# A fused attention and expert kernel: rows of the next units fetched in the middle of a unit, a block's steps further apart, the third stage's tables in later and smaller pieces

## The chip, the cores and the metric

The kernel runs on one core of a Trainium2 chip. The core has five engines with an instruction queue each: PE (TensorE, matmuls and transposes), DVE (VectorE), ACT (ScalarE), POOL (GpSimd) and SP (SyncE, which here only issues DMAs). An engine takes its instructions in the order of the program and waits on semaphores. The metric is the device time of one execution in microseconds; lower is better.

## What is computed

Two layers on x (2048 tokens, 256 features), each with a residual. Layer norms stand ahead of each part. S is 1601 context rows.

```python
# first layer
x += softmax((Q(ln x) K(ctx)^T * tau + delta) / 4) V(ctx) @ Wo.T   # 16 heads of 16
x += expert_w[argmax(router)] (ln x) * max(softmax(router))        # 8 experts, top 1
# second layer
score = ln(x) @ W_a @ ctx^T, only in a window of +-16 around p_t   # rows outside: -1e9
x += tanh(concat(softmax(score) * gauss @ ctx, ln x) @ W_c.T)
x += slot mixing of ln x: 64 slots, top 8 routing, GRU, slot attention
```

## The kernel before

**First stage** (lines 305 to 738) makes the keys, the values and the queries of the first block of 512 tokens.

**Second stage** (lines 740 to 932) is attention. It runs through 16 units: four blocks of 512 tokens (lb) by four groups of four heads (g), `u = lb * 4 + g`. A unit has 13 iterations i, one for each tile of 128 context rows. An iteration has two slots (pl). A slot writes scores of two heads into PSUM with four matmuls (L904), and ACT takes the exponential (L909). An iteration later `weigh` (L866) multiplies the four exponentials with the values into `acc` (L870); after tile 12 of a unit `finish` copies `acc` to `osb` (L808) and adds steps to a list, `later`.

Before a unit's scores are made, the largest score of each query is searched in bfloat16, so that it can be taken off within the score matmul. `look` (L774) is called four times an iteration and places pieces of that search: PE writes one or two groups of 402 scores (L257; a "take" of 1 uses the one-bank buffer `small`, a take of 2 the two-bank buffer `big`), and DVE reduces them to a maximum (L262). The search runs 8 slots ahead (`LEAD`). When its 64 groups are done, `least` and `turned` bring the maxima by PE, ACT and four small DMAs (L292) into rows of `qt`.

Other work goes in between as steps of `later`, one at a time, after an iteration's `weigh`:

- `block(lb)` (L470): the next block's `stats` (layer norm statistics on DVE, the power on POOL, L102), two times `norm` (L107), two times `turned` (four transposes, L240, and a copy), two times `project` (four matmul passes, L498) with `seconds` (two DVE operations, L303, and `store_queries`, four DMAs to DRAM rows, L216); then `residual` on POOL (L601).
- `finish`: `rows` (transposes and a division, L820); after the fourth group also two `turned` and two `out_half` (L845, and the sum into x, L850).
- `bias` once, in unit 0, and `block_0` near the end: the expert stage's first norm and router.

The gap between two steps is set by the length of the list (L919): the next may start 2 slots later when more than 5 steps wait or the step has a second half, otherwise 4. `busy_to` makes `look` use takes of 2 alone for a short time after a step. Block lb+1 is appended at tile 2 of the first unit of block lb (L890).

The rows of queries come back from DRAM by DMA on SP: `fill(u)` (two DMAs into `qt`, two into `ql`) and `fill_search(u)` (two into `qb`). There are three buffers of `qt` and `ql` (`nq = 3`) and two of `qb`. They are issued behind a unit, for the unit three later (L926 to L929).

**Third stage** (lines 935 to 1553): loads on SP and POOL queues (L953 to L988), then experts for blocks of tokens. `experts(lb)` (L1054) makes 16 pairs a block: two experts at a time for a tile of tokens (four matmul passes, L1064, into one of four y banks), added by two DVE operations (L1071). After each pair `aside(3)` advances up to three generators in turn: `front` (the next block's norm, transposes and router), `window` (the tables of the second layer's window, made once from the two numbers `pt` and `slen`), `slots` (the slot parts that do not depend on x), and for each finished block `windowed` and `weights`. `window` runs to its next `yield`: its first piece is ten DVE instructions (L1095 to L1113) and a gather by POOL (L1115), the second makes `posr`, `inr`, `gr`, `negw`, the third `nout`, `ins`, `gs`. Seven empty yields follow, then its matmuls: `eT`, the sum over all rows outside the window (`out_ps`, 13 row tiles, L1177), `oT`, `m` and `ew`.

Of the kernel before, what the change touches and what calls it, by code (L numbers as in the profile page):

```python
# [25 lines left out]
NLB = T // LB  # L26
TPB = LB // P
NS = (S + P - 1) // P
# [3 lines left out]
NG = 4  # L32
# [30 lines left out]
def body(ctx: ExitStack, tc: tile.TileContext, a: dict, out: bass.AP):  # L63
# [41 lines left out]
    def layer_norm_apply(src, dst, i, stats, rows=P):  # L105
        mv, rstd = stats
        nc.vector.tensor_scalar(  # L107
            dst[:, i, :], src[:, i, :], mv[:rows, i, 0:1], rstd[:rows, i : i + 1],
            ALU.subtract, ALU.mult,
        )  # L110
# [69 lines left out]
    with (  # L180
# [9 lines left out]
        nq = 3  # L190
# [42 lines left out]
        def small():  # L233
            return ps_a.tile([P, LB], F32, tag="pa1", name="a1_ps")
# [4 lines left out]
        def turn(ps, src, t, c, n=P):  # L239
            nc.tensor.transpose(ps[:, t * P : (t + 1) * P], src[:, t, c * P : c * P + n], ident)  # L240
# [64 lines left out]
        with (  # L305
# [164 lines left out]
            def block(lb):  # L470

                xb = x_sb[:, lb * TPB : (lb + 1) * TPB, :]

                rstd_of = []

                def stats():
                    rstd_of.append(layer_norm_stats(xb, TPB))

                yield stats
                for half in range(2):  # L480
                    def norm(half=half):
                        for t in range(half * 2, half * 2 + 2):
                            layer_norm_apply(xb, xn, t, rstd_of[0])

                    yield norm
                for c in range(2):
                    def turned(c=c):
                        ps = small()
                        for t in range(TPB):
                            turn(ps, xn, t, c)  # L490
                        nc.scalar.copy(xnT[:, c, :], ps)

                    yield turned
                for n in range(2):
                    def project(n=n):
                        ps = small()
                        for c in range(2):
                            nc.tensor.matmul(  # L498
                                ps, wq[:, c, n * P : (n + 1) * P], xnT[:, c, :],
                                start=c == 0, stop=c == 1,  # L500
                            )
                        b = bq[:, n : n + 1]
                        if lb == 0:
                            (all_parts if n else pick_queries)(ps, b)
                            return
                        for t in (one_two, hi_lo):
                            first_part(t[0], ps, b)

                        def seconds():
                            for t in (one_two, hi_lo):  # L510
                                second_part(t[1], t[0], ps, b)
                            store_queries(lb, n)

                        return seconds

                    yield project
# [82 lines left out]
            def residual(lb):  # L599
                for t in range(lb * TPB, (lb + 1) * TPB):  # L600
                    nc.gpsimd.tensor_tensor(x_sb[:, t, :], x_sb[:, t, :], bo, ALU.add)  # L601

            def fill_search(u):

                lb, g = divmod(u, NG)
                fetch_rows(qb[u % 2], q_rows[1][lb % 2][g // 2], g)

            def fill(u):

                lb, g = divmod(u, NG)  # L610
                rows = q_rows[0][lb % 2][g // 2]
                fetch_rows(qt[u % nq], rows, g)
                for h in range(2):
                    src = head_rows(rows, g, h).rearrange("(e w) l s -> e w l s", w=W)
                    nc.sync.dma_start(
                        raw(ql[u % nq][h * HR : h * HR + W * E : W]), src[:, W - 1]
                    )
# [122 lines left out]
        with (  # L740
# [25 lines left out]
            NU = NLB * NG  # L766

            LEAD, NSL = 8, 2 * NS  # L770
            searches, held, begun = [], [], []
            taken, last, at, busy_to = 0, 1, 0, 0

# [26 lines left out]
            later, free = [], 0  # L800
# [65 lines left out]
            def weigh(u, i, acc, es):  # L866
# [7 lines left out]
                if i == NS - 1:  # L874
                    later.extend(finish(u, acc))

            before = None
            for u in range(NU):
                acc = None
                for i in range(NS):  # L880
                    if (u, i) == (0, 4):
                        later.insert(0, bias)
                    if (u, i) == (0, 1):
                        for lb in range(2, NLB):
                            load_x(nc.sync, lb)
                    if (u, i) == (2, 0):
                        load_experts()
                    if (u, i) == (NU - 3, 2):
                        later.extend(block_0())
                    if u % NG == 0 and i == 2 and u // NG + 1 < NLB:  # L890
                        later.extend(block(u // NG + 1))
                        later.append(lambda lb=u // NG + 1: residual(lb))
                    n = srows(i)
                    es = []
                    assert i or len(begun) >= u, (u, begun)
                    ready = bool(later)
                    for pl in range(2):
                        slot = (u * NS + i) * 2 + pl
                        look(slot)
                        ps = two()  # L900
                        for k, q in enumerate((qt, ql)):
                            for h in range(2):
                                rows = slice(h * HR, h * HR + NROW)
                                nc.tensor.matmul(  # L904
                                    ps[:n, h, :], kt[u % NG][rows, pl, i * P : i * P + n],
                                    q[u % nq][rows, pl, :], start=k == 0, stop=k == 1,
                                )
                        e = esp.tile([P, 2, LB], F32, name="es")
                        nc.scalar.activation(e[:n], ps[:n], AF.Exp)  # L909
                        es.append(e)  # L910
                    look(slot + 0.5)
                    if before is not None:
                        weigh(*before)

                        look(slot)
                    if ready and slot >= free:

                        rest_of_it = later.pop(0)()
                        free = slot + (2 if len(later) > 5 or rest_of_it else 4)  # L919
                        busy_to = at + (9 if rest_of_it else 2)  # L920
                        if rest_of_it:
                            later.insert(0, rest_of_it)
                    if i == 0:
                        acc = ps_o.tile([P, LB], F32, tag="po", name="acc")
                    before = (u, i, acc, es)
                if u + nq < NU:  # L926
                    assert u % NG != 1 or len(later) < 2, (u, len(later))
                    fill(u + nq)
                    fill_search(u + nq)  # L929
            weigh(*before)  # L930
            while later:
                later.pop(0)()
# [5 lines left out]
    slot = ctx.enter_context(tc.tile_pool(name="slot", bufs=1))  # L938
# [152 lines left out]

    def window():

        slen = late.tile([P, 1], F32, name="slen")
        nc.vector.tensor_copy(slen, slen_i)  # L1095
        lo = late.tile([P, 1], F32, name="lo")
# [7 lines left out]
        base_i = late.tile([P, 1], I32, name="base_i")  # L1104
        nc.vector.tensor_copy(base_i, base)
        nc.vector.tensor_copy(base, base_i)

        at_i = late.tile([NW, 1], I32, name="at_i")
        nc.gpsimd.iota(at_i, pattern=[[0, 1]], base=0, channel_multiplier=1)
# [10 lines left out]
        def in_window(pos, n, name):  # L1120

            t = late.tile([P, n], F32, name=name)
            nc.vector.tensor_scalar(t, pos, lo, None, ALU.is_ge)
            nc.vector.scalar_tensor_tensor(t, pos, hi, t, ALU.is_le, ALU.mult)
            return t

        def gauss(pos, n, name):
            t = late.tile([P, n], F32, name=name)
            nc.vector.tensor_scalar_sub(t, pos, pt)
            nc.vector.tensor_tensor(t, t, t, ALU.mult)  # L1130
            nc.scalar.activation(t, t, AF.Exp, scale=-1.0 / 128.0)
            return t
# [4 lines left out]
        posr = late.tile([P, NW], F32, name="posr")  # L1137
        nc.vector.tensor_copy(posr, posr_i)
        nc.vector.tensor_scalar_add(posr, posr, base)
        inr = in_window(posr, NW, "inr")  # L1140
        gr = gauss(posr, NW, "gr")
        neg = late.tile([P, 1, NK], F32, name="negw")
        nc.vector.tensor_scalar(neg[:, 0, :NW], inr, -1.0, 3e38, ALU.add, ALU.mult)
# [9 lines left out]
        nc.gpsimd.iota(row_i, pattern=[[P, NS]], base=0, channel_multiplier=1)  # L1153
        row = late.tile([P, NS], F32, name="row")
        nc.vector.tensor_copy(row, row_i)
        ins = in_window(row, NS, "ins")
        gs = gauss(row, NS, "gs")
        nc.vector.tensor_scalar(ins, ins, -1.0, 1.0, ALU.mult, ALU.add)
# [1 line left out]
        one = late.tile([1, 1], F32, name="one")  # L1160
        nc.gpsimd.memset(one, 1.0)

        for _ in range(7):
            yield
        eT = late.tile([P, 2, NW], F32, name="eT")
        gET = late.tile([P, 2, NK], F32, name="gET")
# [466 lines left out]
```

## Time and profile before

| | before |
|---|---|
| median of three runs | 1055.93 us (1054.44 to 1056.26) |
| the profiled execution's own time | 1057.95 us |
| its span, first to last instruction | 1056.1 us |
| mean granted PE clock | 0.978 |
| busy: PE, DVE, ACT, POOL | 949.2, 745.1, 519.7, 71.8 us |
| chain that ended last | PE 67%, DVE 25%, issue 4%, DMA 2% |
| first stage | 0 to about 93 us |
| attention, first exponential to last `osb` copy | 93.3 to 769.6 us |
| third stage | 769.5 us to the end |

The span is what the profile sees of the core's instructions; the execution's own time is 1.9 us longer. The page's slices show the whole at a glance, each digit a tenth of 26.4 us:

```profile
PE   7788778999988999998899999899979999999885
DVE  6456868888877888877788887875044749585744
PEclk8998999999999999999999999989998999999998
```

PE is busy almost throughout, DVE second. A pass of a float32 matmul is an instruction of its own in the profile, so that a matmul written once in the code counts twice there. "Idle before" in a row names what ended the engine's last wait. A wait on several semaphores is put down to the one that came last.

### The profile page before, as it was taken

The numbers are of one execution on the slowest core, as the hardware profiler recorded it, in microseconds if no ns is written. First come the engines' busy times: TensorE is split into PE (matmuls) and PEld (weight loads), VectorE is DVE, ScalarE is ACT, GpSimd is POOL, SyncE is SP. The second block draws the span as 40 slices with busy tenths as digits, with TensorE's granted clock in tenths as the row PEclk, the third lists the DMA queues.
The fourth block names the chain that finished last, engine by engine and source line by source line (L and its number), as shares of the span: only waits on it lengthen the run. The fifth ranks groups of instructions, "written<-read, shape, count | busy, mean of one in ns | idle before, by whom it ended". The sixth has DMA issues, their size and how long they took to land.

```text
span 1056.1 us, 14900 instructions
## 1 busy us (share of the span) xinstructions
PE 949.2 (90%) x5822; PEld 443.7 (42%) x5822; DVE 745.1 (71%) x1407; ACT 519.7 (49%) x614; POOL 71.8 (7%) x96
## 2 busy tenths in 40 slices
PE   7788778999988999998899999899979999999885
PEld 3234333444443344443343444443334464545543
DVE  6456868888877888877788887875044749585744
ACT  1423556676756666657566766557820012121430
POOL 4000200000010000000000000000030102121210
PEclk8998999999999999999999999989998999999998
DMA  4764721310102201101211011000080000000002
GB/s 161 158 163 94 150 73 46 110 29 2 29 1 79 68 2 28 29 1 39 81 28 29 2 29 29 1 2 1 2 223 7 1 0 1 1 1 0 1 1 80
DMA packets 32277, 46.98 MB, mean 44 GB/s; under 512 B 6411, under 2 KB 21268, under 8 KB 31950
## 3 DMA queue, kind: packets, MB, share of 16 engines
q1 hardware_dynamic: 30478, 43.65, 15.3%
q10 hardware_dynamic: 1232, 1.61, 0.4%
q8 instruction: 46, 0.75, 0.3%
q0 software_dynamic: 496, 0.76, 0.3%
q14 instruction: 25, 0.20, 0.1%
HBM read 26.77 MB, written 14.04 MB: 39 GB/s over the span
## 4 chain that ended last, share of the span: by engine, by line
PE 67%; DVE 25%; issue 4%; DMA 2%; POOL 1%; ACT 1%; SPq 0%; POOLq 0%; DVEq 0%; ACTq 0%
PE acc L870 18%; PE s_ps L904 14%; DVE mx L262 12%; PE a_ps L257 11%; PE y_ps L1064 7%; DVE xn L107 2%; DVE x_sb L1071 2%; PE a_ps L498 2%; DVE ln_stats L96 1%; PE o_ps L1250 1%; PE a_ps L845 1%; PE a_ps L240 1%; PE s_ps L627 1%; PE a_ps L284 1%; PE x_ps L461 1%
## 5 line engine op out<-in xcount | busy, mean ns | idle before, releaser
L262 DVE TENSOR_REDUCE mx<-a_ps 128x2 f32<-128x804 f32 (+1 forms) x637 | 490.9, 806 | 125.6 <-PE a_ps L257 118.9
L909 ACT ACTIVATE es<-s_ps 128x1024 f32<-128x1024 f32 (+1 forms) x416 | 408.3, 1022 | 204.5 <-PE s_ps L904 201.4
L257 PE MATMUL a_ps<-kb,qb 50*128 50x402 bf16 x992 | 219.5, 342 | 49.0 <-DVE mx L262 40.1
L904 PE MATMUL s_ps<-qt,kt 52*128 52x512 f32 (+1 forms) x832 | 238.2, 521 | 1.5 <-DMA qt<-nT 1.4
L870 PE MATMUL acc<-es,v 128*32 128x512 f32 (+1 forms) x1664 | 225.5, 613 | 0.0
L257 PEld LDWEIGHTS <-qb 50*128 50x128 bf16 x1024 | 77.8, 94 | 296.0 <-issue 282.2
L904 PE MATMUL s_ps<-ql,kt 52*128 52x512 f32 (+1 forms) x832 | 191.8, 396 | 0.0
L904 PEld LDWEIGHTS s_ps<-qt,kt 52*128 52x128 f32 (+1 forms) x832 | 98.1, 189 | 32.0 <-ACT es L909 16.7
L904 PEld LDWEIGHTS s_ps<-ql,kt 52*128 52x128 f32 (+1 forms) x832 | 104.0, 187 | 0.7
L1064 PE MATMUL y_ps<-expert_wT_sb,xT 128*128 128x512 f32 x192 | 89.8, 598 | 0.0
L102 POOL TENSOR_TENSOR ln_rstd<-ln_ve,mhalf 128x2 f32<-128x2 f32 (+2 forms) x28 | 21.1, 754 | 754.2 <-DVE ln_ve L100 752.9
L1071 DVE SCALAR_TENSOR_TENSOR x_sb<-y_ps,r_gate,x_sb 128x256 f32<-128x256 f32 x96 | 46.3, 482 | 32.5 <-PE y_ps L1064 30.7
L870 PEld LDWEIGHTS acc<-es,v 128*32 128x32 f32 (+1 forms) x1664 | 33.1, 108 | 42.2 <-issue 40.5
L1064 PEld LDWEIGHTS y_ps<-expert_wT_sb,xT 128*128 128x128 f32 x192 | 34.1, 191 | 31.9 <-issue 30.8
L1027 ACT COPY xT<-tr_ps 128x512 f32<-128x512 f32 (+1 forms) x28 | 13.4, 494 | 53.3 <-PE tr_ps L1024 53.3
L107 DVE TENSOR_SCALAR xn<-x_sb,ln_mv,ln_rstd 128x256 f32<-128x256 f32 x64 | 33.9, 573 | 1.3 <-POOL ln_rstd L102 1.3
L819 DVE RECIPROCAL rec<-a_ps 128x16 f32<-128x16 f32 x16 | 4.0, 252 | 42.6 <-PE a_ps L240 42.6
L1064 PE MATMUL y_ps<-expert_wT_sb,xnT 128*128 128x512 f32 x64 | 32.6, 637 | 0.0
L1024 PE MATMUL tr_ps<-ident,xn 128*128 128x128 f32 x88 | 17.8, 300 | 10.7 <-DVE xn L107 10.7
L96 DVE BATCH_NORM_STATS2 ln_stats<-x_sb 128x6 f32<-128x256 f32 x64 | 23.3, 413 | 3.4 <-POOL x_sb L1258 3.4
L1071 DVE SCALAR_TENSOR_TENSOR x_sb<-y_ps,gate,x_sb 128x256 f32<-128x256 f32 x32 | 15.5, 483 | 14.0 <-PE y_ps L1064 13.3
L997 PE MATMUL busy_ps<-xnT 128*128 128x512 bf16 x95 | 24.2, 387 | 0.0
(347 smaller groups left out, 724.7 us busy)
## 6 DMA issues: line engine op xcount, KB each, us to landing
qt<-q_rows SPq DMA_DIRECT2D x32, 192.0 KB
q_rows<-qhi SPq DMA_DIRECT2D x8, 512.0 KB
qb<-q_rows SPq DMA_DIRECT2D x30, 96.0 KB
kt<-expert_wT_sb SPq DMA_DIRECT2D x24, 100.5 KB
q_rows<-qp SPq DMA_DIRECT2D x8, 256.0 KB
q_rows<-qlo SPq DMA_DIRECT2D x8, 256.0 KB
ql<-q_rows SPq DMA_DIRECT2D x32, 64.0 KB
expert_wT_sb<-in_expert_wT SPq DMA_DIRECT2D x1, 2048.0 KB
```

Source lines behind the costliest of these rows:

```text
L96: nc.vector.bn_stats(stats[:rows, i, :], src[:, i, :])
L102: nc.gpsimd.tensor_tensor(rstd[:rows, :n], ve[:rows, :n], mhalf[:rows, :n], ALU.pow)
L107: nc.vector.tensor_scalar(dst[:, i, :], src[:, i, :], mv[:rows, i, 0:1], rstd[:rows, i : i + 1], ALU.subtract, ALU.mult,)
L257: nc.tensor.matmul(ps[:, k, :CH], qb[u % 2][rows, pl, t * P : (t + 1) * P], kb[g][rows, pl, c * CH : (c + 1) * CH], start=True, stop=True,)
L262: nc.vector.tensor_reduce(flat[:, n : self.n], ps[:, : self.n - n, :CH], AX.X, ALU.max)
L498: nc.tensor.matmul(ps, wq[:, c, n * P : (n + 1) * P], xnT[:, c, :], start=c == 0, stop=c == 1,)
L870: nc.tensor.matmul(acc[HP * j : HP * (j + 1), :], v[:n, i, h * VW : h * VW + HP], es[j // 2][:n, j % 2, :], start=i == 0, stop=i == NS - 1,)
L904: nc.tensor.matmul(ps[:n, h, :], kt[u % NG][rows, pl, i * P : i * P + n], q[u % nq][rows, pl, :], start=k == 0, stop=k == 1,)
L909: nc.scalar.activation(e[:n], ps[:n], AF.Exp)
L997: nc.tensor.matmul(calm[0].rearrange("p e d -> p (e d)"), xnT[:, 1, :P].bitcast(BF16)[:, 1::2], xnT[:, 0, :].bitcast(BF16)[:, 1::2], start ...
L1064: nc.tensor.matmul(ps.rearrange("p e d -> p (e d)"), xT[:, c, tok], ew[:, c, pair * 2 * D : (pair + 1) * 2 * D], start=c == 0, stop=c == 1,)
L1071: nc.vector.scalar_tensor_tensor(xb[:, t, :], ps[:, k, :], gate[:, t, e : e + 1], xb[:, t, :], ALU.mult, ALU.add,)
```

## The change

Three things are changed.

1. `fill` and `fill_search` move from behind a unit to its iteration i = 6, from unit 1 on, and fetch for the unit two later (`u + nq - 1`).
2. The limit above which steps follow each other by 2 slots goes from 5 waiting steps to 9 (`LATE`). Block 1 is appended at tile 8 of unit 0 and not at tile 2; blocks 2 and 3 stay where they were, at tile 2 of units 4 and 8.
3. `window` begins with five empty yields, has four more yields between its pieces, and four instead of seven empty ones ahead of its matmuls.

```diff
-            LEAD, NSL = 8, 2 * NS
+            LEAD, NSL, LATE = 8, 2 * NS, 9
...
+            blocks_at = {(0, 8): 1, (NG, 2): 2, (2 * NG, 2): 3}
...
-                    if u % NG == 0 and i == 2 and u // NG + 1 < NLB:
-                        later.extend(block(u // NG + 1))
-                        later.append(lambda lb=u // NG + 1: residual(lb))
+                    if (u, i) in blocks_at:
+                        lb = blocks_at[u, i]
+                        later.extend(block(lb))
+                        later.append(lambda lb=lb: residual(lb))
+                    if u and i == 6 and u + nq - 1 < NU:
+
+                        assert u % NG != 2 or len(later) < 2, (u, len(later))
+                        fill(u + nq - 1)
+                        fill_search(u + nq - 1)
...
-                        free = slot + (2 if len(later) > 5 or rest_of_it else 4)
+                        free = slot + (2 if len(later) > LATE or rest_of_it else 4)
...
-                if u + nq < NU:
-                    assert u % NG != 1 or len(later) < 2, (u, len(later))
-                    fill(u + nq)
-                    fill_search(u + nq)
...
     def window():
+        for _ in range(5):
+            yield
         slen = late.tile([P, 1], F32, name="slen")
...
         nc.vector.tensor_copy(base, base_i)
+        yield
...
         nc.vector.tensor_scalar_add(posr, posr, base)
+        yield
         inr = in_window(posr, NW, "inr")
+        yield
         gr = gauss(posr, NW, "gr")
...
         nc.vector.tensor_copy(row, row_i)
+        yield
         ins = in_window(row, NS, "ins")
...
-        for _ in range(7):
+        for _ in range(4):
             yield
```

As the changed program is laid out, the steps fall as follows, written as (unit, iteration). Block 1: before, stats at (0,2), norms at (0,3) and (0,5), turned at (0,7) and (0,9), projects at (0,11) and (1,1); after, stats (0,8), norms (0,10) and (0,12), turned (1,1) and (1,3), projects (1,5) and (1,8). Block 2, and block 3 four units on: before, out_half (4,5) and (4,6), stats (4,7), norms (4,8) and (4,9), turned (4,11) and (5,0), projects (5,2) and (5,5), rows (5,10); after, out_half (4,5) and (4,7), stats (4,9), norms (4,11) and (5,0), turned (5,2) and (5,4), projects (5,6) and (5,9), rows (6,1). In the third stage `window`'s first DVE instruction stands behind the sixth pair of the first expert block and not behind the first.

## The prediction, on record before the changed kernel ran

> **What bounds the kernel now.** I read the chain of waits first: PE holds 67% of it and DVE 25%, so PE is the engine to follow and DVE is what stops it. Then I cut the span into stretches, one per attention unit and then the start of the third stage, and looked for the ones where PE is idle. Columns: stretch, length, then busy time with instruction count for PE, PEld, DVE, ACT and POOL, the granted PE clock, DMA share, GB/s.
>
> ```profile
> 93.30:149.90 56.60, 45.70 (x297) 19.69 (x298) 43.21 (x70) 28.52 (x31) 6.74 (x10) 0.94 0.57 118
> ...
> 442.20:488.10 45.90, 42.44 (x311) 20.12 (x309) 36.79 (x61) 27.98 (x31) 4.07 (x5) 1.00 0.07 18
> 488.10:534.20 46.10, 40.97 (x293) 17.48 (x290) 35.11 (x50) 29.61 (x34) 0.00 (x0) 1.00 0.20 69
> ...
> 573.70:611.90 38.20, 36.25 (x284) 16.00 (x281) 32.65 (x48) 26.70 (x29) 0.00 (x0) 1.00 0.08 21
> ...
> 778.00:793.00 15.00, 7.25 (x25) 4.00 (x25) 10.70 (x43) 0.93 (x3) 5.30 (x14) 0.83 1.01 272
> 793.00:797.50 4.50, 4.50 (x10) 2.33 (x10) 1.36 (x4) 0.59 (x1) 0.00 (x0) 0.50 0.00 1
> ```
>
> Row four is unit 11, without a block's steps: PE idle 2.0 of 38.2 us. Rows two and three are units 8 and 9, which carry a block: longer by 7.7 and 7.9 us, but idle only 3.5 and 5.1, so most of their length is the steps' own matmuls. Unit 0 (row one) idles 10.9. The outlier is the fifth row: PE busy 7.25 of 15 us, then 4.5 us at half clock. The timeline there:
>
> ```profile
> 776.72 0.15 DVE L1095 CAST slen<-slen_i 128x1 f32<-128x1 int32 x1 [2.54 <-DMA slen_i<-in_slen]
> ...
> 778.00 0.15 DVE L1097 TENSOR_SCALAR lo<-pt_b 128x1 f32<-128x1 f32 x1 [1.13 <-DMA pt_b<-in_pt]
> ...
> 779.56 1.99 PE L845 MATMUL a_ps<-WoT_sb,aT 128*128 128x256 f32 x8 [1.53 <-DVE x_sb L850]
> ...
> 789.14 0.80 PE L1024 MATMUL tr_ps<-ident,xn 128*128 128x128 f32 x2 [3.72 <-DVE xn L107]
> ...
> 792.45 0.80 PE L1024 MATMUL tr_ps<-ident,xn 128*128 128x128 f32 x2 [2.50 <-DVE xn L107]
> ```
>
> DVE stands in front of two small loads (2.54 and 1.13 us) because window()'s first instructions come early in its queue; the last attention block's L850 is behind them, then the layer norm. PE's three gaps are 1.53, 3.72 and 2.50 us, 7.75 together. The clock records show half speed from 787.9 to 798.1; an expert pair there took 3.41 us in the chain of waits, 1.88 elsewhere.
>
> **Third stage: the later tables.** The piece order of the changed kernel on DVE is now: stats, pair 2, stats, L850, pair 3, L850, two norms, pair 4, two norms, pairs 5 and 6, and only then slen. I walk it with the rows' durations (pair on DVE 1.00, stats of two tiles 1.25, L850 0.69, norm of two tiles 0.73; pair on PE 1.88, L845 group 1.97, four transposes 1.06, router 1.85).
> Until 774.2 nothing differs. DVE: pair 2 to 775.2, stats to 776.5, L850 when PE's first L845 group ends (777.17), so to 778.0. PE's second L845 group starts at 778.05 instead of 779.56 and ends at 780.05. Then pair to 781.9, gate transposes to 782.5, pair to 784.4. The norms need POOL's rstd. POOL issues its thirteen loads until 780.57, clears xn and takes 0.73 us twice: 781.5 and 782.3. DVE: norms to 782.3, pair 4 to 783.3, norms to 784.0, before PE asks at 784.4. From there PE is fed: transposes 785.5, pair 787.3, transposes 788.4, pair 790.2, router to 792.0. Before, the router ended at 801.27. Difference **-9.2 us**: the 7.75 of gaps, and the rest half clock.
> Given back? The tables' PE work (output sum 5.71, the rest 2.7 us) goes from the first expert block into the next, the same amount. Its 26 DVE instructions up to gs sum to 4.9 us; the pieces are 0.4 to 1.2 us beside PE pairs of 1.88, of which DVE uses 1.00. Cover is thus 0.88 per pair and the four y banks lend one or two pairs. Without that cover it would be 4.9 us back. POOL's gather now waits for at_i at about 794, with posr and row queued behind it; POOL's next rstd is needed in the next expert block only. From the third expert block on PE's order is the same, so the gain is carried to the end. I take -9.2, bounds -4.3 and -10.
>
> **Attention: rows fetched in the middle.** fill(u+2) at key tile 6 of unit u replaces fill(u+3) at the end of unit u: the same six DMAs 6.5 tiles later in program order. What releases them is the last matmul on the old qt, at the end of unit u-1, in both. SP's queue shows that they are issued then (unit 5 ends at 364.6; its last use of the old qt is just before 362.2):
>
> ```profile
> 362.23 0.80 SPq L226 DMA_DIRECT2D qt<-q_rows  x2
> 363.12 1.34 SPq L615 DMA_DIRECT2D ql<-q_rows  x2
> 364.52 1.04 SPq L226 DMA_DIRECT2D qb<-q_rows  x2
> ```
>
> SP runs ahead of PE's place, so the issue time stays. What they are moved past on SP: in unit 1 the stores of block 1's queries now come after fill(3), and the four expert loads before fill(4). The experts' 2 MB, issued at 197.5, kept the DMA engines busy to about 204.7, some 7 us; put ahead, fill(4) lands that much later, near 206, and its search starts near 222. In blocks 2 and 3 nT of one search goes ahead of the second store. The cost is 0, hidden by the 18 slots of 1.47 us (26 us) between issue and search. If SP were held at its place in the program, 6 slots (8.8 us) would stay for 4.3 us of issue plus the landing; upper bound 2 us a unit for 13 units.
>
> **Attention: steps further apart.** I measure an iteration from its first acc matmul to the next one's:
>
> ```profile
> 247.23 1.07 PE L870 MATMUL acc<-es,v 128*32 128x512 f32 x8
> ...
> 249.73 1.06 PE L870 MATMUL acc<-es,v 128*32 128x512 f32 x8
> ```
>
> That is 2.50 us. An iteration's search takes sort them: takes of 2,1,2 give this 2.50; 1,2,1 give 2.71; 1,2,1,2 give 3.34; with a step inside, the trace has 3.3 (turned), 4.95 (out_half), 4.12 (stats), 6.13 (project), 3.65 (seconds), 4.26 (a lone norm beside 1,2,1,2). I placed the new order's steps and takes and gave each iteration the length of its like.
> Blocks 2 and 3: tiles (4,6) to (6,12) took 110.6 us. New: unit 4's seven, 2.5+5.0+2.5+5.4+3.2+3.0+2.5 = 24.1; unit 5, with two projects at 6.75 and 6.0, two seconds at 3.65 and two lone turned at 3.4, 46.1; unit 6, now with two rows steps, 39.1. Sum 109.3: -1.3 each. PE's idle time there is 10.7 us, but the 1.2 us that a project and the 1.3 that stats cost are waits of PE for DVE inside that step, and go wherever it goes.
> Block 1: tiles (0,2) to (2,5) took 112.2; new: unit 0 42.0, unit 1 50.7, unit 2's six 18.4, sum 111.1: -1.1.
> Units 13 and 14: the same steps in other tiles, 64.9 before; 61.7 after plus whichever half-clock spells return (4.8 us before): +0.5, between -3 and +1.6. Together **-3.2**, bounds -7 and +2. The new norm and stats places match one row each, which is why these are wide.
>
> **A rule against it.** The Trainium skill, TensorE: Matmul & The Clock Gate, section "HAM oscillation — how this bites in real kernels", says in effect: avoid PE-idle gaps over about 3.4 us. By it only the hole before 793 costs clock, and steps spread over more iterations, each stopping PE for 1.3 us or less, cost none. The trace is harsher: the records show half clock from 678.6 to 682.0, right after one 1.09 us gap behind a lone norm, and that iteration took 4.07 instead of 2.50. By the rule the spread adds 0 and the sum below stays 1043.6; by the row each lone norm or stats adds 1.6, and the change makes about ten such places: 1059.6. But other stretches as idle kept full clock, so I take 0 and put the row into the range.
>
> **The sum.** The profiled execution took 1057.95 us (span 1056.1, 1.9 around it), 2.0 above the median of the runs, 1055.93. -9.2 - 3.2 + 0 = -12.4: 1045.6 against its own time, 1043.6 against the median; I say 1044.
>
> **Rivals.** *Attention gives nothing:* the steps' waits move along and one or two half-clock spells eat the 3.2. For it: PE is already busy for 89 to 92% of block units. Time 1055.9 - 9.2 = 1047. *The tables' stall moves:* at the new place DVE has route and pair work too (0.19 us times seven, plus 0.68 and 1.00, beside one PE pair), so all 4.9 us return. For it: DVE busy 33.1 of 50 us from 830 on. Against: four banks. Time 1055.9 - 4.3 - 3.2 = 1048.4. *Fetch held at its place:* it doesn't do what it says then; it is hidden anyway unless landing takes over 4.5 us. *Slower, by clock:* half-clock spells in the attention stage at 1.6 us (678.6) to 3.2 (699.1, after the router's small matmuls), about 2.4 each. Six more would be 14.4 and turn -12.4 into a loss; seven give 1061. For it: ten new lone places. Against: cut in the clock records' steps of 3.41 us, the attention stage has a dozen stretches with PE busy under 70%, and one such spell.
>
> **How the numbers follow.** Forecast 0.60 (1044); attention nothing 0.17 (1047); stall moves 0.12 (1048); more gained than read 0.04 (1040); slower 0.07. A measurement tells 0.2%, 2.1 us, from no change. The first four make 0.93; of it 0.04 is for both losses with some spells on top, which end between 1054 and 1058: faster 0.89, same 0.04, slower 0.07. The range goes from the likeliest less its bound, 1039.5, to both losses together with one spell, 1051.5.
>
> **What would show it.** Right: no gap over 1 us on PE from 769 to 800, full clock there, router end near 792; blocks' three units within 131 to 129 us; fills issued at the end of the unit before. Wrong: DVE waiting for slen late, half clock in several block units, PE waiting for a DMA on qb or qt, or gaps near the output sum in the second expert block.

## The result, and the profile after

The changed kernel takes 1040.93 us (median of 5 runs, 1038.75 to 1048.27) against 1055.93 (5 runs, 1054.44 to 1058.84): a ratio of 0.9875, 95% interval 0.9852 to 0.9898. It is faster by 15.0 us where 12.4 were forecast. The execution that was profiled is the longest of the five, 1048.27 us (span 1046.4), and the one with the lowest clock (0.973), so its trace shows only 9.7 us less than the trace of before.

First the stretches, in the columns of before: unit 0, unit 9, unit 11, and the 15 and 4.5 us that lie as far behind the last `osb` copy (767.64, before 769.57) as the stretches 778.0 to 797.5 did.

```profile
93.20:144.30 51.10, 43.32 (x286) 19.14 (x288) 40.70 (x69) 26.55 (x27) 5.88 (x8) 0.90 0.63 136
489.50:537.50 48.00, 42.67 (x296) 18.05 (x293) 35.61 (x49) 30.06 (x35) 1.52 (x2) 0.96 0.19 63
576.50:614.60 38.10, 36.12 (x283) 15.98 (x281) 32.59 (x48) 26.67 (x28) 0.00 (x0) 1.00 0.07 20
776.10:791.10 15.00, 14.91 (x61) 8.67 (x60) 9.29 (x30) 1.98 (x4) 5.17 (x12) 1.00 0.97 266
791.10:795.60 4.50, 4.50 (x11) 2.01 (x11) 4.17 (x17) 0.00 (x0) 0.14 (x4) 1.00 0.06 16
```

The fourth row is the one that mattered: PE is busy for 14.91 of 15 us where it was 7.25, and the fifth runs at full clock. Unit 9 (second row) has grown from 46.1 to 48.0 us, at a clock of 0.96 where before had 1.00. Part of that is its steps, which are not those of before: unit 5 of the changed kernel has the same steps at full clock and took 46.5. The timeline of the third stage:

```profile
767.64 0.59 ACT L808 COPY osb<-acc 128x512 f32<-128x512 f32 x1 [1.15 <-PE acc L870]
...
781.73 1.12 PE L1028 MATMUL tr_ps<-ident,xn 128*128 128x128 f32 x4
...
784.41 0.60 PE L1028 MATMUL tr_ps<-ident,xn 128*128 128x128 f32 x4
...
785.53 0.14 DVE L1102 CAST slen<-slen_i 128x1 f32<-128x1 int32 x1
...
786.56 1.85 PE L155 MATMUL r_ps<-router_wT_sb,xT 128*128 128x8 f32 x16
```

Neither the transposes nor `slen` carry a wait in brackets now, and the router ends at 788.41, which is 20.8 us after the last `osb` copy; before it was 31.7. Not all of these 10.9 us are kept: from the `osb` copy to its end the third stage takes 278.7 us in this execution and 286.5 before, 7.8 less. The clock records show half clock from 842.1 for 6.8 us and from 889.9 for 6.8, where before has none between 798.1 and 1047.3. The fetches of rows on SP:

```profile
365.10 0.80 SPq L226 DMA_DIRECT2D qt<-q_rows  x2
365.99 1.34 SPq L615 DMA_DIRECT2D ql<-q_rows  x2
367.38 1.05 SPq L226 DMA_DIRECT2D qb<-q_rows  x2
```

They go out 2.1 us ahead of the end of unit 5 (367.2); before, 2.4 us ahead of it. Nothing moved in the changed kernel. And the place where unit 9 lost time, behind a lone norm:

```profile
491.43 1.00 DVE L262 TENSOR_REDUCE mx<-a_ps 128x2 f32<-128x804 f32 x1 [0.38 <-PE a_ps L257]
492.34 0.73 DVE L107 TENSOR_SCALAR xn<-x_sb,ln_mv,ln_rstd 128x256 f32<-128x256 f32 x2
492.48 0.35 PE L257 MATMUL a_ps<-kb,qb 50*128 50x402 bf16 x2 [1.09 <-DVE mx L262]
...
494.47 1.93 PE L870 MATMUL acc<-es,v 128*32 128x512 f32 x8
```

PE stands for 1.09 us until DVE has reduced a take of 2. DVE was not late: it had idled 0.38 us for that take. As I read it, PE's next matmuls are a take of 2 as well (`busy_to` asks for that after a step), so they need the same two-bank buffer, and a norm gives PE nothing else to do in between. From 493.9 the records show half clock for 3.4 us, and eight passes of L870 take 1.93 us where they take 1.06 elsewhere. The iteration that follows, 2.50 us at full clock, takes 3.81 (494.47 to 498.28).

### The profile page after: what moved, and what is told of

It reads as the page before. It is cut to its first block, busy times and chain, and to the rows that moved or that the text cites. A ratio compares the mean times of both kernels' runs of the same rounds, so it can differ in the third digit from the quotient of the medians.

```text
span 1046.4 us, 14890 instructions
## 1 busy us (share of the span) xinstructions
PE 953.8 (91%) x5814; PEld 446.9 (43%) x5822; DVE 744.5 (71%) x1408; ACT 518.5 (50%) x614; POOL 72.2 (7%) x96
## 4 chain that ended last, share of the span: by engine, by line
PE 70%; DVE 22%; issue 4%; DMA 2%; POOL 1%; ACT 1%; SPq 0%; POOLq 0%; DVEq 0%; ACTq 0%
PE acc L870 19%; PE s_ps L912 14%; PE a_ps L257 12%; DVE mx L262 11%; PE y_ps L1068 8%; DVE xn L107 2%; PE a_ps L498 2%; PE a_ps L240 1%; DVE x_sb L1075 1%; PE o_ps L1261 1%; DVE ln_stats L96 1%; PE a_ps L845 1%; PE s_ps L627 1%; PE a_ps L284 1%; PE x_ps L461 1%
## 5 line engine op out<-in xcount | busy, mean ns | idle before, releaser
L262 DVE TENSOR_REDUCE mx<-a_ps 128x1 f32<-128x402 f32 (+1 forms) x638 | 491.8, 806 | 122.4 <-PE a_ps L257 115.3
L870 PE MATMUL acc<-es,v 128*32 128x512 f32 (+1 forms) x1664 | 226.7, 616 | 0.0
L1068 PE MATMUL y_ps<-expert_wT_sb,xT 128*128 128x512 f32 x192 | 94.4, 624 | 0.0
L870 PEld LDWEIGHTS acc<-es,v 128*32 128x32 f32 (+1 forms) x1664 | 33.1, 108 | 42.3 <-issue 40.0
L1031 ACT COPY xT<-tr_ps 128x512 f32<-128x512 f32 (+1 forms) x28 | 13.5, 493 | 52.1 <-PE tr_ps L1028 52.1
L1068 PE MATMUL y_ps<-expert_wT_sb,xnT 128*128 128x512 f32 x64 | 29.6, 597 | 0.0
L601 POOL TENSOR_TENSOR x_sb<-x_sb,bo 128x256 f32<-128x256 f32 x16 | 11.9, 768 | 129.4 <-DVE bo L763 95.7
L262 DVE TENSOR_REDUCE mx<-s_ps 128x2 f32<-128x804 f32 x16 | 15.9, 993 | 5.4 <-PE s_ps L257 5.4
```

What stands on the lines that cost most here:

```text
L262: nc.vector.tensor_reduce(flat[:, n : self.n], ps[:, : self.n - n, :CH], AX.X, ALU.max)
L870: nc.tensor.matmul(acc[HP * j : HP * (j + 1), :], v[:n, i, h * VW : h * VW + HP], es[j // 2][:n, j % 2, :], start=i == 0, stop=i == NS - 1,)
L1068: nc.tensor.matmul(ps.rearrange("p e d -> p (e d)"), xT[:, c, tok], ew[:, c, pair * 2 * D : (pair + 1) * 2 * D], start=c == 0, stop=c == 1,)
```

## The experiments

"Third stage" times are counted from the last `osb` copy, "half clock" is summed from the clock records of the profiled execution. Medians are of 4 to 22 runs; before measured 1054.5 to 1055.7 beside them.

**Part 3 alone.** The kernel before with the diff of `window` only.

> The kernel before with the third part of the change alone: the tables begin five pairs later and in more pieces; the attention stage is that of before. By the theory (three PE gaps of 7.75 us and the half clock behind them go, nothing is given back) it takes 1055.9 - 9.2 = 1046.7, and if the 1.7 us by which the router ended still earlier than forecast in the changed kernel's profile belongs to this part, 1045. By the rival that the attention stage brought most of the 15 us and the third stage gave part back, it takes 1049 or more. Its first expert block's router should end about 21 us after the last osb copy, as in the changed kernel (20.8), and not 31.7.

Measured 1042.16 us, ratio 0.988 (0.9864 to 0.9896), so -12.7. The router ends at 20.7 us.

**Parts 1 and 2 alone.** The diff of the second stage only.

> The kernel before with the first two parts of the change: rows fetched in the middle, 9 instead of 5 waiting steps, block 1 at tile 8; the tables as before. By the theory of the prediction -3.2: 1052.7; what the whole change brought beyond the forecast (15.0 against 12.4) would make it up to -5.8: 1050. By the rival that attention gives nothing (half-clock spells eat it), 1055.9 within 1 us. The three gaps of PE after the last osb copy (1.5, 3.7, 2.5 us) must be there.

Measured 1050.41, ratio 0.9958 (0.9943 to 0.9973): -4.4. Alone, the attention part does gain, and the three gaps are there (1.58, 3.72 and 2.51 us). But the two parts' 4.4 and 12.7 add to more than the whole change's 15.0, and the attention stage of its profile has 17.1 us of half clock.

**Part 1 alone.**

```diff
-            LEAD, NSL, LATE = 8, 2 * NS, 9
+            LEAD, NSL, LATE = 8, 2 * NS, 5
-            blocks_at = {(0, 8): 1, (NG, 2): 2, (2 * NG, 2): 3}
+            blocks_at = {(0, 2): 1, (NG, 2): 2, (2 * NG, 2): 3}
```

(on top of the kernel of parts 1 and 2)

> The kernel before with the first part alone: fill and fill_search for unit u+2 at tile 6 of unit u; steps and blocks at their old places, tables as before. By the theory nothing: the same six DMAs are released by the same matmul, so 1055.9 within 1 us, and the first qt issue of a unit stays within 1 us of the end of the unit before. By the rival (SP held at its place, or stores queued before the rows cost or save something) it is 2 us or more off, either way.

Measured 1054.75, ratio 1.000 (0.999 to 1.001). The fetch's place in the program is worth nothing in itself; its use is that the steps may be placed later. But the time came out right although the issue times did not stay. Where a block's queries are stored ahead of tile 6, the fetch stands behind the stores (L216) on SP. First this kernel, then before:

```profile
334.26 0.45 SPq L216 DMA_DIRECT2D q_rows<-qlo  x1
334.80 1.24 SPq L226 DMA_DIRECT2D qt<-q_rows  x2
```

```profile
316.16 0.79 SPq L226 DMA_DIRECT2D qt<-q_rows  x2
```

That is 18.6 us later; two other units have 13.5 and 18.7. PE's waits for `qt` stay at 1.4 us in all. In the changed kernel the steps are later too, and the fetches go out ahead of these stores.

**Later, in the old pieces.**

```diff
     def window():
+        for _ in range(5):
+            yield
         slen = late.tile([P, 1], F32, name="slen")
```

> The kernel before with only five empty yields ahead of the tables: later, but in the three old pieces (ten, then five, then seven small DVE instructions at once) and seven empty yields behind. By the theory the place is what matters (DVE no longer stands before two loads in front of the last block's sum), so it gains what the tables' whole part gains, within 0.7 us: about 1046. By the rival that the pieces matter (a longer piece than the 0.88 us that a pair leaves delays the y banks), each old piece of 1.5 to 2 us costs PE up to 1 us, three of them: 1048 to 1050.

Measured 1039.25, ratio 0.9865 (0.984 to 0.989): -15.6. (The three old pieces have ten, seven and nine DVE instructions.) The place alone brings everything that part 3 brings; more pieces add nothing.

**In more pieces, at the old place.**

```diff
     def window():
-        for _ in range(5):
-            yield
         slen = late.tile([P, 1], F32, name="slen")
```

(on top of part 3 alone)

> The kernel before with the pieces of the tables alone: four more yields between them and four empty ones behind, none ahead, so slen still comes behind the first pair. By the theory that the place is what matters, DVE still stands before the two loads ahead of the last block's sum (2.5 and 1.1 us) and PE's gap of 1.5 us stays; only the gather's address and the later pieces move out of the layer norm's way, at most half of the 7.75 us of gaps: 1051 to 1055. By the rival that small pieces matter, it gains most of the tables' part (12.7): 1043 to 1046.

Measured 1051.11, ratio 0.9973 (0.9961 to 0.9985): -3.8. The router ends at 27.3 us; PE's gaps are 3.5 and 1.3 us and not 1.5, 3.7 and 2.5.

**The two loads first**, everything else as before: this takes away what the prediction held to be the cause.

```diff
+    slen_i = late.tile([P, 1], I32, name="slen_i")
+    nc.sync.dma_start(slen_i, a["slen"].partition_broadcast(P))
+    pt = late.tile([P, 1], F32, name="pt_b")
+    nc.sync.dma_start(pt, a["pt"].partition_broadcast(P))
     ctx_sb = late.tile([P, NS, D], F32, name="ctx_sb")
...
-    slen_i = late.tile([P, 1], I32, name="slen_i")
-    nc.gpsimd.dma_start(slen_i, a["slen"].partition_broadcast(P))
-    pt = load_rows(late, "pt")
```

> The kernel before with nothing moved but the two loads of slen and pt: they are issued on SP ahead of the 1.6 MB of context rows and not on POOL beside them, so that they land some 2 us after the last osb copy and not 7 to 8. By the theory that DVE's stand before these loads makes the gaps, the stand goes and with it the first gap (1.5), half of the second and third and the half clock behind: what stays is the tables' own DVE work of some 4 us ahead of the norms, hidden or not. It gains 6 to 11 of the tables' 12.7: 1044 to 1049. By the rival that the tables' own DVE instructions, or POOL's load queue ahead of rstd, make the gaps, it gains 0 to 3: 1052 to 1055.

Measured 1053.34, ratio 0.9984 (0.9972 to 0.9996): only -1.6. DVE no longer waits for the loads, and the hole is there all the same. In its timeline:

```profile
771.35 0.69 DVE L850 TENSOR_TENSOR x_sb<-x_sb,a_ps 128x512 f32<-128x512 f32 x1 [2.19 <-PE a_ps L845]
...
774.13 0.69 DVE L850 TENSOR_TENSOR x_sb<-x_sb,a_ps 128x512 f32<-128x512 f32 x1 [2.09 <-PE a_ps L845]
...
775.53 0.15 DVE L1112 CAST at<-at_i 64x1 f32<-64x1 int32 x1 [0.72 <-POOL at_i L1110]
...
779.04 0.22 DVE L1139 CAST posr<-posr_i 128x64 f32<-128x64 int32 x1 [1.01 <-POOL posr_i L1137]
...
781.98 0.80 PE L1025 MATMUL tr_ps<-ident,xn 128*128 128x128 f32 x2 [4.01 <-DVE xn L107]
```

DVE stands twice for POOL. The tables begin with constants that POOL makes (`at_i`, `posr_i`, `row_i`). `at_i` stands in POOL's queue behind all its loads and behind the first rstd; `posr_i` stands behind the second rstd, which needs stats that DVE makes only after its wait for `at_i`.

**And POOL's constants first.** The three `iota` lines moved up, ahead of the load of `b1`; the tables' 26 DVE instructions stay ahead of the second norm.

> The kernel before with the two loads first, as in the last such experiment (1053.3, PE gaps of 4.0 and 2.5 us ahead of the two pairs of transposes), and POOL's three iotas ahead of its other loads, so that DVE never stands for POOL within the tables (0.72 us for at_i and 1.01 for posr there). The tables' DVE instructions stay where they were, ahead of the norms. By the theory that the rest of the hole is the tables' own DVE work in the queue ahead of the norms, it gains about 1.7 more: 1051 to 1052, gaps 2.5 and 2.5. By the rival that standing for POOL makes the hole, it gains most of the rest: 1044 to 1047.

Measured 1045.97, ratio 0.9911 (0.9895 to 0.9928): 7.4 us less than with the loads alone. The theory that the rest is the tables' own DVE work is wrong here, and its rival's number right.

```profile
767.28 0.58 ACT L808 COPY osb<-acc 128x512 f32<-128x512 f32 x1 [1.15 <-PE acc L870]
...
772.62 0.14 DVE L1116 CAST at<-at_i 64x1 f32<-64x1 int32 x1
...
775.02 0.19 DVE L1141 CAST posr<-posr_i 128x64 f32<-128x64 int32 x1
775.13 0.68 DVE L850 TENSOR_TENSOR x_sb<-x_sb,a_ps 128x512 f32<-128x512 f32 x1
...
777.94 0.68 DVE L850 TENSOR_TENSOR x_sb<-x_sb,a_ps 128x512 f32<-128x512 f32 x1
...
783.22 0.66 PE L1031 MATMUL tr_ps<-ident,xn 128*128 128x128 f32 x2 [1.28 <-DVE xn L107]
...
787.59 1.85 PE L155 MATMUL r_ps<-router_wT_sb,xT 128*128 128x8 f32 x16
```

No wait on either table row, one gap of 1.28 us left, and the router ends 789.44 - 767.28 = 22.2 us after the `osb` copy. More than the two waits has changed. With the loads alone, DVE takes `at`, pair 2, its stats and `posr` behind both L850, and idles 2.19 and 2.09 us for PE ahead of these; with the iotas first it has taken all four by 775.2 and idles ahead of neither. POOL's loads are not the difference: its first rstd starts 10.9 us after the `osb` copy with the loads alone and 11.2 here.

So of the 11 us between 31.7 and 20.7, 2.4 went with the loads (to 29.3). 7.1 went with POOL's late constants: the two waits, the order on DVE that came with them, and the half clock behind (6.8 us of it in the profile of the loads first, none here). How the 7.1 divide among these is not shown. The last 1.5 are what the tables in front of the norms still cost; the gap of 1.28 is in them.

**Old pieces with the changed attention.** The whole change, with `window` as in "later, in the old pieces".

> The changed kernel with the tables five pairs later but in their old three pieces (attention as changed). If the two parts add (4.4 and 15.6 in the runs) it takes 1054.9 - 20 = 1035; if splitting is worth nothing either way and the difference of the two tables variants (1042.2 and 1039.3) is chance in half-clock spells, it takes what the changed kernel takes, 1038 to 1041.

Measured 1041.78, ratio 0.9876 (0.9851 to 0.99). It does not add up to 1035: what the attention part brings alone is gone again. Its profile has 20.5 us of half clock in the attention stage, with spells at 321, 478 and 492 us.

**Block 1 early again.** On the changed kernel `(0, 2): 1` in place of `(0, 8): 1`.

> The changed kernel with block 1 back at tile 2 of unit 0; fetch and 9 waiting steps stay. By the prediction's sum block 1's new place is worth 1.1 us, so 1042; by the rival that unit 0 (idle 10.9 of 56.6 us before) is where the attention part gains, it loses most of 4.4: 1045.

Measured 1045.5, ratio 0.9892 (0.9866 to 0.9918), which overlaps the changed kernel's interval. Two of its six runs took 1040.2 and 1040.5 at a clock of 0.983 and 0.982, four 1045.3 to 1046.4 at 0.975 to 0.977. The median is the rival's 1045, but with two groups of runs so far apart, what block 1's place is worth is not settled by it.

**5 waiting steps again.**

```diff
-            LEAD, NSL, LATE = 8, 2 * NS, 9
+            LEAD, NSL, LATE = 8, 2 * NS, 5
```

> The changed kernel with 5 instead of 9 as the limit of waiting steps; fetch in the middle, block 1 at tile 8, tables as changed. By the theory that wider steps are worth 1.3 us in each of blocks 2 and 3 and cost as much in half clock (the lone norms at (5,0) and (9,0)), the clock rises from 0.981 to 0.984 or so and the time stays within 1.5 us of the changed kernel's: 1039.5 to 1042.5. By the rival that the limit carries the attention part's 4.4 us, it takes 1044 or more at the clock of the changed kernel.

Measured 1040.7, ratio 0.9858 (0.9834 to 0.9883), mean clock of its runs 0.9845 against 0.981. The theory's case: with the rest of the change in place the wider steps are worth nothing.

**The holes filled.** Behind each `norm` and `stats` step of the attention stage, four matmuls that compute nothing.

```diff
-                        look(slot)
                         ps = two()
+                        if quiet and searches:
+                            src = qb[searches[0].u % 2][:, 0, :LB]
+                            for _ in range(4):
+                                nc.tensor.matmul(
+                                    ps[:, 0, :], src[:, :P], src, start=True, stop=True
+                                )
+                        quiet = False
+                        look(slot)
...
-                        rest_of_it = later.pop(0)()
+                        step = later.pop(0)
+                        quiet = step.__name__ in ("norm", "stats")
+                        rest_of_it = step()
```

> The changed kernel with four extra bfloat16 matmuls (into a score bank that the real scores then overwrite) behind each of the twelve norm and stats steps of the attention stage, where PE stands 1.1 to 1.3 us for DVE: they fill the hole and compute nothing. By the theory that the steps' new places cost clock (in the profiles 17 to 24 us of half clock in attention with the new spacing against 7 to 14 in most with the old; the spell near 490 us, behind the lone norm at (9,0), is in all four kernels with the new spacing and in none of six with the old), the spells behind these steps go: mean clock from 0.981 to 0.986 or more, 1037 to 1039. By the rival (spells fall anywhere, the holes have no part in it) the clock stays at 0.981 and the time at 1041, or up to 3 us more if the extra matmuls hold up the takes.

Measured 1039.06, ratio 0.9847 (0.983 to 0.9864), mean clock 0.987; the interval overlaps the changed kernel's. The same lone norm in its profile:

```profile
483.96 1.04 PE L911 MATMUL s_ps<-qb 128*128 128x512 bf16 x4
484.07 0.99 DVE L262 TENSOR_REDUCE mx<-a_ps 128x2 f32<-128x804 f32 x1 [0.37 <-PE a_ps L257]
484.98 0.73 DVE L107 TENSOR_SCALAR xn<-x_sb,ln_mv,ln_rstd 128x256 f32<-128x256 f32 x2
485.11 0.35 PE L257 MATMUL a_ps<-kb,qb 50*128 50x402 bf16 x2
...
486.94 1.06 PE L870 MATMUL acc<-es,v 128*32 128x512 f32 x8
```

The four fill 1.04 us of the hole, and the eight passes of L870 take 1.06. Three of the twelve places pay for it: iterations (4,11), (8,11) and (13,7) take 3.68 us each, at full clock, where the changed kernel has 2.98, 2.98 and 2.88. Between 93 and 762 us one spell is left (694.6, 6.8 us). The clock in 40 slices, first of the changed kernel, then of this one:

```profile
PEclk8998979999999999999999999999999989899998
```

```profile
PEclk9999999999999999999999999999999999999999
```

The attention stage, from the first exponential (with the spell that lies across it) to the last `osb` copy, takes 670.7 us here, 674.4 in the changed kernel and 676.3 before, with 6.8, 27.3 and 20.5 us of half clock.

**Filled, with the old pieces.** The last kernel, with `window` as in "later, in the old pieces".

> The filled kernel (1039.1) with the tables five pairs later in their old three pieces. In the profiles the old pieces left the third stage's last expert pair at 197.8 and 198.1 us after the last osb copy, the small ones at 200.8 to 205.3, since PE stood less for the softmax behind (0.9 against 1.2 to 2.0 us) and fell to half clock less there. By the theory that this is real: 1036 to 1037, last pair near 198, less than 4 us of half clock in the third stage ahead of its end. By the rival that the pieces make no difference and spells fall by chance: 1038 to 1041.

Measured 1037.25 (1034.12 to 1041.22), ratio 0.9836 (0.9812 to 0.9861): the fastest median of the study, 3.7 us under the changed kernel, though the intervals overlap a little. The last expert pair ends at 199.5 us of the third stage, with one spell of 3.4 us (882.9): between the two theories. So it is not shown that the small pieces cost something at the late place; nowhere there do they bring anything.

## Why the prediction was right, and where it was wrong

The time lies in the range and the larger part is where it was put. Step by step:

- **Third stage, -9.2: right in place, too small, and half wrong in cause.** The part alone brought 12.7, and without its small pieces 15.6. (a) The walk ended the router at 22.4 us after the `osb` copy; it ended at 20.8. The term that was mis-sized is the sum of durations: a pair counts 1.88 in its row, but the next instruction starts 1.72 after it, and the second four transposes took 0.43 from start to start where I took 1.06. From the first pair behind L845 to the router's end I had 12.1 us, the trace has 10.6. The half clock came out too small by as much: the walk left it 1.5 us, but from 787.9 to 798.1 of before PE was busy for 6.45 us at half clock, which is 3.2 too many, and 7.75 + 3.2 is within 0.1 of the 10.9 that was measured. (b) I named DVE's stand before two loads as the cause. The walk was right since it moved all of the tables; but the loads alone are worth 1.6 us, as the loads-first run shows, and POOL's late constants, with the order on DVE that comes with them, most of the rest. The rows were there in the trace of before:

```profile
782.70 0.15 DVE L1111 CAST at<-at_i 64x1 f32<-64x1 int32 x1 [0.42 <-POOL at_i L1109]
...
786.21 0.22 DVE L1138 CAST posr<-posr_i 128x64 f32<-128x64 int32 x1 [1.01 <-POOL posr_i L1136]
```

I did not follow what POOL's queue held ahead of them. (c) "Nothing given back" held for waits: between 755 and 870 us of the changed kernel PE has one gap above 0.5 us, 1.17 at 851. It did not hold for the clock in this execution, with the spells at 842 and 889.9 named above.
- **What is left of the third stage's gain** lies in part at the end. In the profiles of before and part 3 alone, DVE's wait for the first output store:

```profile
1047.63 1.96 DVE L1552 TENSOR_TENSOR o<-x_sb,f_ps 128x512 f32<-128x512 f32 x3 [3.12 <-DMA out_x<-o]
```

```profile
1031.53 2.13 DVE L1559 TENSOR_TENSOR o<-x_sb,f_ps 128x512 f32<-128x512 f32 x3 [1.40 <-DMA out_x<-o]
```

The store itself frees its buffer after 4.3 and 2.6 us. All six profiles with the tables early show 4.2 to 4.6; of those with the tables late, five show 2.3 to 2.6 and three, the changed kernel among them, 4.2 to 4.5. Why stays open; no run was made on it.
- **Fetch in the middle, 0: right in size, half right in cause.** 1.000 in the run. "The issue time stays" holds in the changed kernel, where the steps moved too; with the fetch alone it fails in three units, by up to 18.7 us, and the forecast's other leg, the slack between issue and search, carried it. PE's wait for rows in the changed kernel is 1.4 us in all, as before:

```profile
L912 PE MATMUL s_ps<-qt,kt 52*128 52x512 f32 (+1 forms) x832 | 239.9, 523 | 1.6 <-DMA qt<-nT 1.4
```

- **Steps further apart, -3.2: about right as a schedule (-4.4 alone), wrong in the whole.** At the same 20.5 us of half clock, the attention stage takes 673.5 us with the new spacing (old pieces with the changed attention) and 676.3 and 675.6 with the old (before, iotas first); 5 waiting steps, which has only block 1's new place, takes 674.0 at as much half clock. These are single executions. Block 2's tiles (4,6) to (6,12) took 109.8 us, forecast 109.3, before 110.6. The same tiles of block 3 took 111.3, with one spell in them; block 1's 115.5 (forecast 111.1), with three. Units 13 and 14, forecast +0.5, took 79.5 against 84.3. That was luck: the trace of before has 13.6 us of half clock there and that of after none; iotas first, with the old spacing and none there, took 79.4. So in the profiled pair of executions the stage's 1.9 us (676.3 to 674.4) are not the schedule's gain but what the spells left of it.

  The step that failed is the one where a rule stood against a row: "other stretches as idle kept full clock, so I take 0". The rule (the Trainium skill, TensorE: Matmul & The Clock Gate, section "HAM oscillation — how this bites in real kernels": avoid PE-idle gaps over about 3.4 us) makes a gap of 1.09 us free; the traces do not agree, and the row was right in kind. The lone norm at (9,0) is followed by half clock in all four kernels that have it unfilled (near 490 us), the same norm at (5,0) in two of the four; in the two filled kernels neither is, and the eight others have no spell near 490. The whole attention stage has 17 to 27 us of half clock in those four, 10 to 24 in the seven with the old spacing, which overlap. But not each of the ten places fires, so 16 us was as wrong as 0: filling them is worth 1041.8 - 1038.7 = 3.1 us between the means of the runs of the two kernels, 1.9 between their medians, and the intervals overlap.
- **The rivals.** "Attention gives nothing, half-clock spells eat it" had, as far as is shown, the right mechanism: 1040.93 whole against 1042.16 and 1039.25 with the tables alone. "The tables' stall moves" was wrong. "Slower, by clock" was right that such places can cost; by the filled kernel all of them together cost some 3 us, not clear of noise, where its row would have made 16 of them.

The forecast of 1044 was thus near the result in part by luck, because two errors partly cancel: a third stage that gained 3 to 6 us more, an attention part that gained less once the rest was there. How much less is known only to within some 2 us.

## What to carry to other kernels

Before calling a wait on a load the cause of a stall, follow the queue of every engine that the late engine talks to: two queues with small instructions that need each other can cost several times what the longest bracket shows, since work that was ready stands behind the one that waits. Sum a walk from start to start and not from durations. And when small steps are moved on an engine that a second one waits for, ask where the second will stand a microsecond, and have independent work for it there.

## What the runs showed of the hardware

A gap of 1.1 us on PE, in an iteration with PE busy for some 3.2 of 4.4 us, can be followed by half clock for 3.4 us or more: at six of the eight lone norms at (5,0) and (9,0) in the four kernels that have them unfilled. In the changed kernel itself (5,0) at 323.7 kept full clock and (9,0) at 492.5 lost it. What decides between the two is not shown.

Nor is a gap needed. In the changed kernel's profile PE is busy without a break, at full clock, for the 7.1 us in front of a spell (length, then PE's busy time; the clock is the last but two):

```profile
835.00:842.10 7.10, 7.10 (x46) 5.34 (x45) 2.67 (x9) 0.81 (x2) 0.00 (x0) 1.00 0.00 0
842.10:848.90 6.80, 6.80 (x11) 2.92 (x10) 3.19 (x10) 0.42 (x1) 0.00 (x0) 0.50 0.00 0
```

There the router's and the window's small matmuls stand in front (L155 and L1232). Two other kernels, block 1 early and 5 waiting steps, have a spell at the same place. Its cause stays open.

The spread between runs of one kernel goes with the clock: the five runs of the changed kernel go from 1038.75 at a mean clock of 0.985 to 1048.27 at 0.973, nearly on a line (correlation -0.99), and so do those of most others (-0.8 to -1.0). Where the spells fell is known only for the profiled ones. Four matmuls that compute nothing, put in such gaps, kept the clock at all four lone norms of the two filled kernels and cost nothing there; at three other places they cost 0.7 to 0.8 us each.
